# A four-layer graph network on one Trainium2 core: bias rows in two parts, late query rows on GpSimd, and the first block's chunks counted before layer 0

## The chip, the cores and the metric

The kernel runs on one core of one Trainium2 chip. Its time is the device time of one execution in microseconds (us), and of several executions the median is given. A core has five engines that run side by side, each through its own list of instructions in order: TensorE (PE in the profile; its weight loads are the rows PEld), VectorE (DVE), ScalarE (ACT), GpSimd (POOL) and SyncE (SP), which here only issues transfers. GpSimd issues transfers too, on a queue of its own. An engine waits for another through semaphores. TensorE's clock can be throttled; the profile shows the granted share.

## The reference

Input are 4096 rows x of 64 features and a 4096 x 4096 matrix adj of zeros and ones (about one in a thousand is a one). Four layers follow each other, each of the form `x = x + layer(max(layernorm(x), 0))`:

```
# layer 0: hyperbolic attention
h = lorentz_linear(h, W, b, scale)          # time column and 63 space columns
q = lorentz_linear(h, Wq, bq, scale_q);  k = lorentz_linear(h, Wk, bk, scale_k)
qm = concatenate([-q[:, :1], q[:, 1:]])
att = adj * sigmoid((2 + 2 * qm @ k.T) / att_scale + att_bias)
support = att @ h
out = support / sqrt(max(|inner(support)|, 1e-8))
# layer 1: weighting by rank
rank = cumsum(adj != 0, axis=1);  deg = rank[:, -1:];  k = minimum(deg, 100)
pos = rank - (deg - k)
w = where(adj != 0 and pos > 0, 0.5 ** (k - pos), 0);  out = w @ (h @ weight) + bias
# layer 2: 1 - 0.1 h - 0.01 * sum(h * (adj @ h))
# layer 3: relu(concatenate([h, adj @ h / max(deg, 1)]) @ W.T)
```

`lorentz_linear` multiplies by a weight, adds a bias row, takes the sigmoid of the first column as "time", and scales the other columns by a factor per row so that the row lies on a hyperboloid.

For layer 1 a row's neighbours are numbered from the last one backwards, so the kernel counts the ones of adj in chunks of 128 neighbours ahead of the numbering inside a chunk.

## The kernel before

**Tiling.** The 4096 neighbours lie in NT = 32 tiles of 128 on the partitions; the 4096 rows that are computed lie in NIB = 8 blocks of IB = 512 columns. For each block the mask, adj as FP8 of 128 x 32 x 512, is loaded by GpSimd's queue (L226, two tiles a load, converted from float32 on the way) and kept for all layers. `load_masks` issues the loads in the order in which layer 0 uses the blocks, 7 down to 0.

**Prologue and first block** (`first_rows_and_block`, L1089). Before any attention the 4096 rows need layer norm, h, q and k. They are done in two groups of 16 tiles (rows 16 to 31 first, then 0 to 15), each described by `before0` (L593) as a list of parts: VectorE means and factors, ScalarE squares and copies out of PSUM, PE transposes (`turned_half`, L678) and products (`product`: a product of bias rows with ones, L719, then products with the weight, L727), GpSimd the time column of h (L854) and of q and k (`qk_times`, L903). The rows of q and k are `qk_rows` (L892): one instruction for eight tiles, the unscaled rows tq times a factor per row, and half u of a group is turned into keys kt by transposes. The first group computes q and k rows on VectorE, the second its key rows on VectorE and its two query rows on GpSimd. Into the same list go the attention tiles of block 7, which needs all keys but only the queries of its own rows (in the first group, upper half), the query transposes of blocks 7 and 6 (`queries_turned`, L989, `queries_laid` on ScalarE), and 40 mask loads.

**The order of all that** is written out: `ORDER` is a tuple of part numbers. `Listing.run` walks through it, gives each part a planned start by planned durations, chooses for PSUM tiles among named places ("pm", "pa", "ps", "pp0", "pp1"), and issues each part on its engine. Where PE has planned idle time ahead of a part, `fill` (called for every part) issues products of ones into a tile `idle` that nobody reads (L1178), 43 at the start and afterwards `int((part.idle - 0.1) / 0.215)`, until the first attention scores. These fillers keep PE busy.

**Bias rows** (`bias_rows`, L493, GpSimd). The three bias vectors of h, q and k (192 columns) are brought as three BF16 parts that add up to float32, in three rounds: cast (L503), multiplication by a selecting column (L505), sum (L507) and remainder (L509), and the last cast to `brow` (L510). Every product of h, q or k starts with `brow`.

**Attention** is a chain for each pair of neighbour tiles: scores on PE (L1053), sigmoid on ScalarE (from PSUM), multiplication by the mask on VectorE (`att`), product with h on PE (L1084, `acc`). After block 7 a loop does blocks 6 to 0; in each turn it issues a score tile, a mask load (`load_masks(1)`), and one step of the jobs pushed earlier: the finished block's rows (`rows0`), the next block's query transposes, and the constants for layer 1 (`count_constants`, L923, pushed once after block 7, where VectorE also clears the tile `lane` and sets its middle column). The pool `pro` of the prologue is closed before the loop, and the masks of blocks 3 to 0 (`mask_b`) take its room.

**Layer 1** starts with `chunks_counted` (L1377), once for blocks 0 to 3 (quad 0) and once for 4 to 7: for each of the 32 chunks, four products of `lane` with a block's mask (L1382), 32 x 512 results each, in four groups of partitions of one PSUM bank. ScalarE copies that to `many`; `numbered` makes of `many` the numbers that go into two mask rows by transfers (L1472), and `counted` (L1495) and `products` (L1530) do the layer. Layers 2 and 3 share their products with adj (`both_layers`, L1627).

Of the kernel before, what the change touches and what calls it, by code (L numbers as in the profile page):

```python
# [10 lines left out]
F32 = mybir.dt.float32  # L11
# [13 lines left out]
D = 64  # L25
# [21 lines left out]
    206, 207, 205, 209, 208, 203, 210, 0, 1, 2, 3, 5, 4, 7, 9, 6, 8, 10, 213, 64, 11, 12, 14, 15,  # L47
    204, 13, 16, 18, 17, 211, 216, 65, 66, 67, 68, 69, 70, 19, 71, 217, 20, 21, 72, 214, 73, 127,
    74, 75, 76, 22, 79, 24, 23, 212, 215, 26, 218, 77, 78, 81, 25, 27, 28, 219, 80, 83, 82, 84,
    29, 31, 30, 85, 87, 33, 34, 32, 86, 221, 89, 88, 35, 36, 220, 37, 38, 90, 91, 222, 39, 40, 92,  # L50
    41, 43, 93, 94, 45, 96, 95, 97, 44, 223, 98, 47, 49, 100, 224, 46, 225, 42, 99, 102, 48, 101,
    50, 51, 52, 53, 60, 103, 104, 106, 56, 108, 110, 54, 57, 128, 105, 55, 61, 107, 129, 109, 111,
    62, 133, 228, 63, 161, 112, 113, 134, 149, 226, 114, 162, 230, 121, 115, 130, 150, 145, 146,
    163, 157, 151, 116, 131, 153, 119, 137, 138, 123, 124, 232, 135, 132, 164, 152, 120, 139, 158,
    136, 122, 154, 169, 147, 233, 173, 155, 170, 177, 174, 229, 165, 117, 231, 234, 156, 166, 58,
    59, 148, 159, 160, 167, 118, 235, 178, 140, 179, 236, 237, 125, 141, 126, 189, 193, 171, 142,
    143, 181, 238, 190, 185, 239, 172, 186, 191, 192, 144, 175, 176, 187, 241, 194, 195, 200, 182,
    201, 197, 240, 180, 198, 183, 184, 202, 242, 199, 196, 188, 227, 168,
# [35 lines left out]
def kernel(  # L94
# [52 lines left out]
    part = cpool.tile([P, QUAD], BF16, name="part")  # L147
    exp_s = cpool.tile([P, 3], F32, name="exp_s")
# [33 lines left out]
    def model(general):  # L182
# [55 lines left out]
        (nc.vector if general else nc.gpsimd).memset(apart_m.bitcast(I32), 0)  # L238
        q_sb = s2a.rearrange("p t k d -> p t (k d)").bitcast(F32)
# [239 lines left out]
        ppro = pool("pp_p", 1, pro_stack, space=PSUM)  # L479
# [13 lines left out]
        def bias_rows():  # L493
            v = vec[:, V_B : V_B + 3 * D]
            sel = pro.tile([P, 3], F32, name="sel" + sfx)
            high = pro.tile([P, 3 * D], BF16, name="high" + sfx)
            left, part = (
                pro.tile([P, 3 * D], F32, name=f"brow_{a}{sfx}") for a in ("left", "part")
            )
            total = pro.tile([P, 3 * D], F32, name="brow_sum" + sfx)  # L500
            nc.gpsimd.tensor_tensor(sel, ident[:, 0:3], ident[:, D : D + 3], ALU.add)
# [8 lines left out]
            nc.gpsimd.tensor_copy(brow, total)  # L510
# [74 lines left out]
        tables, flats = [], []  # L585
# [7 lines left out]
        def before0(todo, gr, bias):  # L593
# [141 lines left out]
            for u in HALF:  # L735
                pairs = [(k, k) for k in range(u * HK, (u + 1) * HK)]
                hs.append(
                    add(
                        "PE", 1.3 if u == 0 else 1.05, product("ht", pairs, 1, W_L, u == 0, "h"), ht[u], *hs, bias,
                        **({"takes": ("ps", "pp1")} if u == 0 else {}),  # L740
                    )
                )
# [124 lines left out]
            def q_out(u):  # L867
                def emit(_):
                    if u == 0:
                        v.tq = buffer("C", "tq", [P, len(HALF), 2, 2 * HK, D])  # L870
# [3 lines left out]
            for u in HALF:  # L874
# [3 lines left out]
                        "PE", 1.3, product("hq", pairs, 2, W_QK, True, f"q{u}"), hq[u],  # L878
# [35 lines left out]
            for u in reversed(HALF):  # L914
                if lead:
                    q = add("DVE", 0.65, qk_rows(u, 0, nc.vector), rq)
                else:
                    q = add("POOL", 1.35, qk_rows(u, 0, nc.gpsimd), rq)
                fq[u] = add("POOL", 0.3, qk_times(u, 0), q)
# [3 lines left out]
        def count_constants():  # L923
# [23 lines left out]
            dve.memset(lane, 0.0)  # L947
            dve.memset(lane[:, NT - 1 : NT], 1.0)
# [140 lines left out]
        def first_rows_and_block():  # L1089
# [4 lines left out]
            bias = add("POOL", 8.1, lambda _: bias_rows(), at=6.5)  # L1094
            made = [before0(listing, gr, bias) for gr in range(len(ROWS))]
# [14 lines left out]

            for ib in (last, last - 1):
# [3 lines left out]
                )  # L1115
                asked[ib] = add(
# [46 lines left out]

            for n in range(0 if general else len(todo) * EARLY // NIB * 5 // 8):
                add("POOL", 0.56, lambda _: load_masks(1), at=2.2 * max(n - 5, 0))

            v.idle = pps[0].tile([P, CG, IB], F32, tag="pp", name="idle" + sfx)
            v.filling = 0

            def fill(part):  # L1170
                if part.engine != "PE" or v.filling is None:
                    return
                if part.form == "scores":
                    v.filling = None
                    return
                for _ in range(int((part.idle - 0.1) / 0.215) if v.filling else 43):
                    v.filling += 1
                    nc.tensor.matmul(  # L1178
                        v.idle[:, v.filling % CG, :], ones,
# [8 lines left out]
        with tc.manual_schedule():  # L1188
            acc, late = first_rows_and_block()
            push(rows0(order0[0], evacuated(order0[0], acc, 0)), 10)  # L1190
            pro_stack.close()
            mp1 = pool("mask_b", 1, side="right")
            for ib in order0[EARLY:]:
                get_mask(mp1, ib)
# [16 lines left out]
            for size in sizes:  # L1211
                now = []
                for n, (ib, g) in enumerate(todo[k : k + size]):
# [10 lines left out]
                    k += 1  # L1224
                    if k == 92 and not general:
# [151 lines left out]
        def chunks_counted(quad, meanwhile):  # L1377

            pc = bank(3 + quad, f"many{quad}")
            for t in range(NT):  # L1380
# [526 lines left out]
```

## Time and profile before

| | |
|---|---|
| median of 3 runs | 569.07 us (568.34 to 570.71) |
| profiled execution | 568.73 us, of it span 567.0 us |
| mean granted clock of TensorE in the span | 0.994 |
| PE busy | 544.4 us, 3335 products |
| VectorE, ScalarE, GpSimd busy | 468.2, 357.1 and 280.2 us |
| first attention score | 44.88 us after the span's start |
| start of the copy that ends layer 0's first block | 79.21 us |
| chunk counting (L1382) | first start 292.2, last start 307.6 us |

The span is the time between the first and the last instruction that the profiler records. Each line of a timeline has the start, the time from the first to the last of its instructions, the engine, the source line, the operation with output and inputs, the shape, and the number of instructions; in square brackets stands the idle time ahead of it on that engine, with what ended it. A chain of waits is followed back from the last instruction: at each step to what released it, or to the instruction ahead of it on its engine. Busy time of PE counts fillers as well, so a busy PE of the prologue does not mean useful work.

### The profile page before, as it was taken

To read this page: it belongs to the slowest core of one execution; us is meant where nothing else is said; L and a number is where in the kernel's file an instruction comes from. 1 tells how busy PE (TensorE), PEld (TensorE's weight loads), DVE (VectorE), ACT (ScalarE), POOL (GpSimd) and SP (SyncE) were. 2 spreads that over 40 slices of the span, in tenths; PEclk is the share of its full clock that TensorE was granted. 3 is DMA by queue.
4 is the path that set the end of the run, shared out by engine and by line. 5 is a ranking of instruction groups with operands and counts; after the bars stand their busy time and mean duration, and the time that the engine had idled before them with its cause. 6 is when DMAs were issued, how large, how long until landed. Compare 5 with 4: busy or idle time off the path is not lost.

```text
span 567.0 us, 9853 instructions
## 1 busy us (share of the span) xinstructions
PE 544.4 (96%) x3335; PEld 279.5 (49%) x3335; DVE 468.2 (83%) x949; ACT 357.1 (63%) x651; POOL 280.2 (49%) x538
## 2 busy tenths in 40 slices
PE   8898999999999999999999999999999999999995
PEld 3553333333333333332334445445454888888884
DVE  5788866899998999898965977778969897789992
ACT  3589577667766758778632888988888332342231
POOL 8626614666867575754345400475644442234332
PEclk9899999999999999999999999999999999999998
DMA  8983992798999999993234255443534778859960
GB/s 141 146 82 32 86 96 20 84 145 142 166 153 148 170 151 172 130 156 97 92 123 136 102 201 163 141 153 116 173 125 149 251 266 294 281 173 328 353 242 21
DMA packets 45612, 87.86 MB, mean 155 GB/s; under 512 B 6272, under 2 KB 24576, under 8 KB 45552
## 3 DMA queue, kind: packets, MB, share of 16 engines
q1 hardware_dynamic: 26112, 69.14, 36.3%
q0 software_dynamic: 18912, 17.77, 33.5%
q8 instruction: 28, 0.46, 0.3%
q10 hardware_dynamic: 528, 0.23, 0.2%
q14 instruction: 32, 0.26, 0.1%
HBM read 135.60 MB, written 1.05 MB: 241 GB/s over the span
## 4 chain that ended last, share of the span: by engine, by line
PE 63%; DVE 14%; POOL 8%; DMA 7%; ACT 4%; issue 3%; SPq 0%; ACTq 0%; DVEq 0%; POOLq 0%
PE acc L1627 15%; PE acc L1084 13%; PE ps L1053 12%; PE acc L1530 8%; PE cnt L1495 8%; DVE att L88 4%; DMA mask<-adjt_dram 3%; DVE ckw L88 2%; POOL mask L226 2%; PE many L1382 1%; DMA s2a<-adjt_dram 1%; DVE s2a L88 1%; PE idle L1178 1%; DMA vec<-vecs_dram 1%; ACT w L88 1%
## 5 line engine op out<-in xcount | busy, mean ns | idle before, releaser
L1053 PE MATMUL ps<-qt,kt 64*128 64x512 f32 x512 | 122.3, 608 | 3.6 <-DVE att L88 3.3
L1084 PE MATMUL acc<-att,fb 128*64 128x512 f32 x512 | 117.1, 599 | 0.5 <-DVE att L88 0.5
L1627 PE MATMUL acc<-s,mask 128*128 128x256 f16 x1024 | 114.0, 273 | 0.4 <-DVE s L88 0.4
L88 ACT ACTIVATE w<-cnt 128x512 int16<-128x512 f32 x187 | 98.7, 606 | 13.0 <-PE cnt L1495 12.1
L1627 PEld LDWEIGHTS <-mask 128*128 128x128 fp8e4 x1024 | 99.8, 98 | 12.9 <-issue 1.0
L88 DVE TENSOR_TENSOR att<-ps,mask 128x1024 f32<-128x1024 f32 x82 | 98.6, 1218 | 9.1 <-ACT ps L88 8.9
L88 DVE SCALAR_TENSOR_TENSOR ckw<-ckw 128x1024 f32<-128x1024 f32 x76 | 96.0, 1273 | 4.0 <-DMA ckw<-adjt_dram 4.0
L88 ACT ACTIVATE ps<-ps,att_c,att_a 128x1024 f32<-128x1024 f32 x82 | 93.8, 1176 | 1.1 <-PE ps L1053 0.7
L88 ACT ACTIVATE att<-ps,att_c,att_a 128x1024 f32<-128x1024 f32 x46 | 54.4, 1203 | 53.0 <-PE ps L1053 48.6
L1053 PEld LDWEIGHTS ps<-qt,kt 64*128 64x128 f32 x512 | 46.1, 186 | 77.5 <-issue 30.2
L226 POOL DMA_DIRECT2D mask<-adjt_dram x128 | 70.3, 562 | 11.0 <-DMA mask<-adjt_dram 9.5
L1495 PE MATMUL cnt<-mask,after 128*128 128x512 fp8e4 x256 | 67.4, 379 | 3.6 <-DMA mask<-two 1.3
L88 DVE TENSOR_TENSOR att<-att,mask 128x1024 f32<-128x1024 f32 x46 | 57.2, 1263 | 14.6 <-ACT att L88 11.2
L1084 PEld LDWEIGHTS acc<-att,fb 128*64 128x64 f32 x512 | 33.8, 136 | 71.6 <-issue 68.4
L1530 PE MATMUL acc<-w,s2a 128*128 128x512 bf16 x256 | 66.2, 379 | 1.2 <-ACT asb L88 1.2
L88 DVE TENSOR_SCALAR w<-cnt 128x512 int16<-128x512 f32 x69 | 46.9, 686 | 23.2 <-PE cnt L1495 22.6
L316 POOL TENSOR_TENSOR rs_a<-rs_y 128x4 f32<-128x4 f32 x48 | 19.1, 398 | 67.6 <-DVE rs_y L88 61.1
L88 DVE SCALAR_TENSOR_TENSOR ck<-ck 128x512 f32<-128x512 f32 x60 | 42.8, 714 | 0.8 <-DMA ck<-adjt_dram 0.8
L1530 PEld LDWEIGHTS <-s2a 128*128 128x128 f16 x256 | 24.7, 98 | 33.6 <-issue 5.6
L88 ACT ACTIVATE xm<-xm,inn 128x64 f32<-128x64 f32 x32 | 10.4, 347 | 47.3 <-DVE high L88 45.1
L1495 PEld LDWEIGHTS <-after 128*128 128x128 bf16 x256 | 24.5, 99 | 31.8 <-issue 2.7
L88 DVE SCALAR_TENSOR_TENSOR s2a<-s2a 128x1024 f32<-128x1024 f32 x22 | 27.7, 1268 | 1.8 <-DMA s2a<-adjt_dram 1.8
(248 smaller groups left out, 611.3 us busy)
## 6 DMA issues: line engine op xcount, KB each, us to landing
ckw<-adjt_dram SPq DMA_DIRECT2D x76, 512.0 KB, 4.4
mask<-adjt_dram POOLq DMA_DIRECT2D x128, 128.0 KB, 8.6
ck<-adjt_dram SPq DMA_DIRECT2D x60, 256.0 KB, 6.0
s2a<-adjt_dram SPq DMA_DIRECT2D x22, 512.0 KB, 4.9
x_sb<-x_dram SPq DMA_DIRECT2D x4, 256.0 KB, 7.5
out_dram<-y POOLq DMA_DIRECT2D x15, 64.0 KB, 3.7
apart_m<-mask SPq DMA_DIRECT2D x16, 16.0 KB, 4.5
mask<-apart_m SPq DMA_DIRECT2D x16, 16.0 KB, 4.7
```

Of the source, the lines that this page charges most:

```text
L88: return op(out, *args, **kw)
L226: nc.gpsimd.dma_start(out=masks[ib][:, g * CG : (g + 1) * CG, :], in_=adjt[ib, g])
L316: nc.gpsimd.tensor_tensor(a, y, y, ALU.mult)
L1053: nc.tensor.matmul(ps[:, c, :], kt[half, g, :], qts[ib][half, :], start=True, stop=True)
L1084: nc.tensor.matmul(acc[c * D : (c + 1) * D, :], lhs[:, t, :], rhs[:, c, :], start=(at == 0), stop=(at == NG - 1), skip_group_check=True,)
L1178: nc.tensor.matmul(v.idle[:, v.filling % CG, :], ones, ones.unsqueeze(1).to_broadcast([P, IB // P, P]), start=True, stop=True, skip_group_ ...
L1382: nc.tensor.matmul(pc[q * NT : (q + 1) * NT, :], lane[:, NT - 1 - t : 2 * NT - 1 - t], masks[quad * QUAD + q][:, t, :], start=(t == 0), st ...
L1495: nc.tensor.matmul(cnt, by, what, start=True, stop=True, skip_group_check=True)
L1530: nc.tensor.matmul(accs[ib], apart_s if t < 0 else both(s2a, t), w, start=(t == NT - 1), stop=False, skip_group_check=True,)
L1627: nc.tensor.matmul(acc[:, to, :, :].rearrange("p k d -> p (k d)"), masks[ib][:, t, c * P : (c + 1) * P], s23[:, t, :, :].rearrange("p k d ...
```

## The change

Four things are changed.

1. `bias_rows` takes a column range. The rows of h (64 columns) are one part of the list, and those of q and k (128 columns) another; h's products wait for the first alone, q's products for the second.
2. Three of the four query rows are taken out of the list: the first group's half 0 (VectorE before) and the second group's two (GpSimd before). They go, with their time column, into `queries_left` and are issued on GpSimd in the first three turns of the loop after block 7, each after that turn's mask load. The pool `pro` is closed after the third; its PSUM part is closed before the loop as it was.
3. The 32 count products of block 7, the first block, are issued by PE before layer 0, into partitions 96 to 127 of the second bank of `idle`: in the place of fillers once 63 of those are counted, and what is left of the 32 ahead of the first query transpose. ScalarE copies them to `first_many` after that transpose. In `chunks_counted` quad 1 then has three products for each chunk in place of four and fills the other 96 partitions of `first_many`. GpSimd clears `lane` at the very start, in place of VectorE in `count_constants`.
4. `ORDER` is a new tuple for the new list. By it the first query row comes ahead of the key rows on VectorE, and on ScalarE the queries of block 7 are laid ahead of the first keys, then `first_many`, then the next keys.

By the order of the changed kernel's instructions, GpSimd issues nine mask loads ahead of the h bias rows (seven ahead of all bias rows before), one between the two parts, and seven after them. PE issues 84 fillers instead of 93. Ahead of the first query transpose stand 18 counts and 17 fillers, where 13 fillers stood ahead of the first key transposes; 4 and 10 counts stand further ahead. The two fillers between the second group's q products are gone.

```
+    nc.gpsimd.memset(lane, 0.0)
+    nc.gpsimd.memset(lane[:, NT - 1 : NT], 1.0)
...
+        first_many = parts.tile([P, IB], BF16, name="first_many" + sfx)
...
-        ppro = pool("pp_p", 1, pro_stack, space=PSUM)
+        ps_stack = ExitStack()
+        ppro = pool("pp_p", 1, ps_stack, space=PSUM)
...
-        def bias_rows():
-            v = vec[:, V_B : V_B + 3 * D]
-            sel = pro.tile([P, 3], F32, name="sel" + sfx)
...
+        def bias_rows(c0, n):
+            cols = slice(c0, c0 + n)
+            v = vec[:, V_B + c0 : V_B + c0 + n]
...
+            if c0 == 0:
+                nc.gpsimd.tensor_tensor(sel, ident[:, 0:3], ident[:, D : D + 3], ALU.add)
...
-            nc.gpsimd.tensor_copy(brow, total)
+            nc.gpsimd.tensor_copy(brow[:, cols], total)
...
                 pairs = [(k, u * HK + k) for k in range(HK)]
                 qs.append(
                     add(
-                        "PE", 1.3, product("hq", pairs, 2, W_QK, True, f"q{u}"), hq[u],
+                        "PE", 1.3, product("hq", pairs, 2, W_QK, True, f"q{u}"), hq[u], bias_qk,
...
             for u in reversed(HALF):
-                if lead:
+                if lead and u == HALF[-1]:
                     q = add("DVE", 0.65, qk_rows(u, 0, nc.vector), rq)
+                    fq[u] = add("POOL", 0.3, qk_times(u, 0), q)
                 else:
-                    q = add("POOL", 1.35, qk_rows(u, 0, nc.gpsimd), rq)
-                fq[u] = add("POOL", 0.3, qk_times(u, 0), q)
+                    queries_left.append((qk_rows(u, 0, nc.gpsimd), qk_times(u, 0)))
...
-            dve.memset(lane, 0.0)
-            dve.memset(lane[:, NT - 1 : NT], 1.0)
...
-            bias = add("POOL", 8.1, lambda _: bias_rows(), at=6.5)
-            made = [before0(listing, gr, bias) for gr in range(len(ROWS))]
+            bias_h = add("POOL", 3.8, lambda _: bias_rows(0, D), at=7.2)
+            bias_qk = add("POOL", 6.2, lambda _: bias_rows(D, 2 * D), at=7.2)
+            made = [before0(listing, gr, bias_h, bias_qk) for gr in range(len(ROWS))]
...
+            def counted_early():
+                g, c = divmod(v.counted, CG)
+                t = first_cols[g] * CG + c
+                top = slice(P - NT, P)
+                nc.tensor.matmul(
+                    v.idle[top, 1, :], lane[:, NT - 1 - t : 2 * NT - 1 - t], masks[last][:, t, :],
+                    start=(v.counted == 0), stop=(v.counted == NT - 1), skip_group_check=True,
+                )
+                v.counted += 1
+
+            def counts_kept(_):
+                if not general:
+                    nc.scalar.copy(first_many[P - NT : P, :], v.idle[P - NT : P, 1, :])
...
+            add("ACT", 0.6, counts_kept, first_turn, idle_place, frees=idle_place)
...
             def fill(part):
-                if part.engine != "PE" or v.filling is None:
+                if part.engine != "PE" or v.filling is None or part is idle_place:
                     return
+                if part is first_turn:
+                    while v.counted < NT:
+                        counted_early()
...
                 for _ in range(int((part.idle - 0.1) / 0.215) if v.filling else 43):
                     v.filling += 1
+                    if v.filling > 63 and v.counted < NT:
+                        counted_early()
+                        continue
                     nc.tensor.matmul(
-                        v.idle[:, v.filling % CG, :], ones,
+                        v.idle[:, 0, :], ones,
...
+            ps_stack.close()
-            pro_stack.close()
-            mp1 = pool("mask_b", 1, side="right")
-            for ib in order0[EARLY:]:
-                get_mask(mp1, ib)
...
                     load_masks(1)
                     k += 1
+                    if queries_left:
+                        for emit in queries_left.popleft():
+                            emit(None)
+                        if not queries_left:
+                            pro_stack.close()
+                            mp1 = pool("mask_b", 1, side="right")
+                            for later_ib in order0[EARLY:]:
+                                get_mask(mp1, later_ib)
...
+            some = QUAD if general or quad == 0 else QUAD - 1
             for t in range(NT):
-                for q in range(QUAD):
+                for q in range(some):
...
-            many[quad] = work1.tile([P, IB], BF16, name=f"many{quad}{sfx}")
-            act.copy(many[quad], pc)
+            if some == QUAD:
+                many[quad] = work1.tile([P, IB], BF16, name=f"many{quad}{sfx}")
+            else:
+                many[quad] = first_many
+            act.copy(many[quad][0 : some * NT, :], pc[0 : some * NT, :])
```

## The prediction

> **What bounds the kernel now.** I read the engines' shares first, then the chain of waits of the first 110 us, then the timeline of that stretch, and last the timeline around the chunk counting, because the change touches only the prologue, the first blocks of layer 0 and that counting.
>
> The engines' shares, from the page:
>
> ```profile
> PE 544.4 (96%) x3335; PEld 279.5 (49%) x3335; DVE 468.2 (83%) x949; ACT 357.1 (63%) x651; POOL 280.2 (49%) x538
> ```
>
> TensorE (PE) is busy nearly always, so what its stream gains or loses early is carried to the end; but in the prologue many of its instructions are fillers (products of ones), so there the chain has to say what matters. The chain of waits, in order of time (start, duration, what):
>
> ```profile
> 12.81 1.78 POOL brow_part L505
> ...
> 15.35 0.70 POOL brow L510
> ...
> 16.09 0.39 PE ps_h L719 x2
> 16.48 1.88 PE ps_h L727 x32
> 18.37 4.61 PE idle L1178 x14
> ...
> 41.08 0.70 DVE kr L892
> ...
> 42.47 0.60 POOL s2a L903
> ...
> 105.33 0.11 DVE lane L88
> ```
>
> Three things stand on it: GpSimd's bias rows (7.28 to 16.05), fourteen fillers of 4.61 us, and from 29.5 to 42.5 the VectorE chain that makes the key and query rows. The timeline shows how PE lies against it (start, busy time, engine, line, count, then the wait ahead and its releaser):
>
> ```profile
> 16.09 0.39 PE L719 MATMUL ps_h<-brow,ones 64*128 64x512 bf16 x2 [1.35 <-POOL brow L510]
> 18.30 4.68 PE L1178 MATMUL idle<-ones 128*128 128x512 bf16 x14
> 37.56 0.60 PE L1178 MATMUL idle<-ones 128*128 128x512 bf16 x2
> 39.31 2.98 PE L1178 MATMUL idle<-ones 128*128 128x512 bf16 x13
> 42.53 0.66 PE L678 MATMUL pt_k<-ident,kr 128*128 128x128 f32 x4 [0.23 <-POOL kr L903]
> 43.70 1.51 ACT L88 COPY qt<-pq 64x256 f32<-64x256 f32 x4
> 44.88 3.23 PE L1053 MATMUL ps<-qt,kt 64*128 64x512 f32 x12 [0.29 <-ACT qt L88]
> 49.94 1.55 POOL L892 TENSOR_TENSOR s2a<-tq,rrq 128x512 f32<-128x512 f32 x1 [4.97 <-ACT att L88]
> 50.50 8.60 DVE L88 TENSOR_TENSOR att<-att,mask 128x1024 f32<-128x1024 f32 x6
> ```
>
> The reader is to see that the thirteen fillers at 39.31 end at 42.29, only 0.23 us before the key rows arrive: the gap was filled to the brim, with no slack for more.
>
> **The change part by part.** The profiled run took 568.73 us: span 567.0 and 1.73 around it. That is 0.34 under the median 569.07; I sum against the span and put the difference on the median. Differences under 0.5% (2.85 us) can hardly be told from none here.
>
> *Bias rows in two parts.* GpSimd now issues nine mask loads before them in place of seven, and two memsets of lane. The queue runs eight loads: the eighth's successor waits for a landing (issue at 20.23, 0.28 after the landing at 19.95). The first load is issued at 1.93 and lands at 9.13, so the ninth starts near 9.5 (0.28 later, 0.1 for the memsets), takes 0.55, and the h part starts near 10.2 instead of 7.28. It has twelve instructions of 64 columns. By the rows of 192 columns (copy 0.34, multiplication 0.77, two-input 0.54) and of 4 columns (0.20), 64 columns cost about 0.24, 0.38 and 0.31: 4 copies, 3 multiplications, 4 two-input, the selection 0.27 and eleven gaps of 0.08 make 4.5 us, so ready at 14.7. Two of the long multiplications took 1.59 and 1.77 beside VectorE's two-input instructions; so the worst bound is no gain, 16.04. I take the middle, 15.35: **-0.7** (0 to -1.4). The second part (eleven instructions of 128 columns, about 7 us by the same rows, after one more load) is ready at 22 to 23.5, and its first user, the q product, stands at 29.88: nothing, covered by 6 us; shorter cover would cost one for one. Behind it on GpSimd seven loads of 0.55 precede the time column of h (26.25 before): 23 + 3.9 is 26.9 at worst, against h rows due near 24 to 25.5; I count nothing, at most +0.7.
>
> *The clock.* The fourteen fillers at 18.30 take 4.68: the first seven stand 0.427 apart, the rest 0.216, so seven ran at half rate, worth 7 x 0.211 = 1.5. Before them PE stood still 1.23 us (12.36 to 13.58) and 1.35 (14.75 to 16.09). The second of these shrinks to about 0.6 with the earlier rows. A lone stop of 1.28 at 309.6 is followed by full rate (four products in 1.02). After the change the stops are nearer to that single one: **-1.5** taken, 0 as the other bound. The Trainium skill ("TensorE: Matmul & The Clock Gate", Part 1: The HAM clock gate) says that the clock falls back only after a whole idle window of about 3.4 us; the stops here are shorter and the rate fell all the same, so the trace disagrees. By the rule there would be nothing to fall and the same sum would stand.
>
> *Two fillers between the last q products* (0.60 at 37.56) are gone: **-0.6**. They stood at a point where PE, not VectorE, decided (no wait ahead of 38.10 but PE's own).
>
> *Counts and fillers ahead of the first query transpose.* The written order now issues there, after the last q product, 18 counts that were left over **and** 17 fillers; the planner counts the idle time of its plan into fillers without taking off the counts. 35 in place of 13. Each streams 512 columns, as a filler does: 0.216. PE's last q product ended at 39.31; less 0.7, 1.5 and 0.6 that is 36.5. 35 x 0.216 = 7.56, so PE is free at 44.07. The query row is ready earlier: it now comes ahead of the key row on VectorE (0.61) and everything before is 2.2 earlier, 43.08 - 2.8 = 40.3. So PE is late by 3.8, and the wait for the query row turns into a wait for fillers. From the query transpose (43.13) to the laid queries' start (43.70) went 0.57: they start at 44.64, take 1.51, and now the first half's keys (0.585) are laid after them: first score at 44.64 + 1.51 + 0.585 + 0.1 = 46.83, against 44.88: **+1.95** in all, with the three gains above already in it. Bounds of a count: 0.216 as above, and 0.43 if a stream of 32 columns lets the clock fall, which no row shows (the counting of L1382 always runs four beside each other).
>
> *The copy of the counts* on ScalarE, 32x512, 0.585 as the cast of `many`, stands ahead of the second half's keys and the first sigmoid: 0 to +0.6, **+0.3** taken, since PE has four score tiles to do meanwhile.
>
> *Query rows moved to GpSimd.* Two rows leave GpSimd's stretch at 49.94 and 52.64, where two mask products took 2.07 each against 1.21 otherwise, and PE waited 0.62 (52.10, for GpSimd's key column behind the row) and 0.50 (55.25, for the second product). VectorE's own row (0.68 at 59.63) goes too. From 55.75 on the chain is PE alone, so only these waits count: **-0.8**, between 0 and -1.1. The three rows now run in the next loop turns, behind mask loads that GpSimd issues there. Whoever waits: query transposes of blocks 3 and lower, far later, and the masks of the last four blocks, whose first is needed after 140 us; nothing. Beside them three mask products can each lose 0.86 (2.6 of VectorE's time); PE's whole wait for mask products in all score tiles is 3.3, so I take 0 and keep +1 as a bound. On this the Trainium skill ("SBUF — State Buffer", SBUF: two separate sides) says that a GpSimd instruction reading SBUF and a VectorE one with two SBUF inputs exclude each other for their whole duration. By that the first of the two products would have lasted 2.2, measured 2.07; the rule speaks against a move to GpSimd, and by it the three rows would cost VectorE up to 3 x 1.0 in the loop.
>
> *Lane's memsets* leave the chain at 105.33 and 105.51, with their gaps **-0.25**.
>
> *Chunk counting in layer 1.* 256 products become 224. One tile's instructions (shortest, median, longest ns, first and last start):
>
> ```profile
> L1382 PE MATMUL many<-mask,lane x256: 379/379/391, 292.2 to 307.6; 128*32 128x512 fp8e4 x128
> ```
>
> and in the timeline what follows them:
>
> ```profile
> 309.61 1.94 PE L1495 MATMUL cnt<-mask,after 128*128 128x512 fp8e4 x7 [1.28 <-DMA mask<-two]
> ```
>
> They start in fours, 3 to 4 ns apart, and the next four 0.216 later: a block's four lanes run beside each other, and three take as long as four, 32 x 0.216 = 6.9. If each product cost its share, 0.054, it would be 32 x 0.054 = 1.7. And behind them PE waits 1.28 for a transfer that starts from the other half's counts. **0** (to -0.4 past that wait).
>
> Sum: +1.95 + 0.3 - 0.8 - 0.25 = **+1.2**: 569.9 for the profiled run, **570.3** on the median.
>
> **The rivals.**
> *The clock falls all the same.* The rows of h need not be earlier, and the stop of 1.23 stays. Then the seven fillers stay at half rate: +1.5, 571.8, and with no earlier bias rows 572.5. For it: the drop has two causes, and one stays.
> *A stream of counts slows itself* (the other side: slower). Counts load only a quarter of the array's columns. If 18 in a row run at 0.43 before the first query, 18 x 0.216 = 3.9 is added on the path: 574.2. It decides from the point where a count takes more than 0.3. Against it: the four-lane counting has full rate, though always four wide.
> *The extra 22 do not lie on the path.* If the query rows come later than I work out (GpSimd busy, VectorE behind), PE's 3.8 of lateness covers them: 570.3 - 3.8 = 566.5. Against it: PE alone already has 7.56 us to do from 36.5.
> *The removed quarter pays.* If a lane costs its share, -1.7: 568.6. Against it: starts in fours, and the 1.28 wait.
>
> **How the numbers follow.** Forecast 0.36 (its own range 569.2 to 572: bias rows ±0.7, copy and waits ±0.5), clock falls 0.26, slow counts 0.18, extra work hidden 0.09, quarter pays 0.11. Slower than 571.9: 0.05 of the forecast's tail, 0.17 of the second, 0.18 of the third, 0.40. Faster than 566.2: 0.06 of the hidden case (with another gain beside it) and 0.02 of the last, 0.08. The rest, 0.52, is within 0.5%. The range leaves out the hidden case and half of the slow counts: 568.0 to 574.2.
>
> **What would show it.** In the profile after: the bias product of h near 15.4; the fillers after h all 0.216 apart; 18 counts and 17 fillers between the last q product and the query transpose, 7.5 us, with no wait of PE behind them; a first score near 46.8; no GpSimd row in the first block, and mask products there of 1.2 only; L1382 as long as before, with 1.3 of waiting behind it. I am wrong if the query transpose waits for its rows, if counts are wider apart than 0.22, if mask products in the next block hold up PE, or if the counting of layer 1 is shorter by over a microsecond with nothing waiting behind it.

## The result, and the profile after

The changed kernel took 570.14 us in the median of 20 runs (568.9 to 572.19), the kernel before 567.53 in 20 runs beside them. The medians lie 2.6 us apart. The ratio over all runs is 1.0032, with a 95% interval of 1.0017 to 1.0047: some 1.8 us slower, and clear of no change, though less than the 0.5% that the prediction took as its bound. The profiled execution took 569.73 us, its span is 568.0.

The lines of its timeline that answer to those shown of before (start, busy time, engine, line, count, wait ahead and its releaser):

```profile
15.52 0.39 PE L725 MATMUL ps_h<-brow,ones 64*128 64x512 bf16 x2 [1.03 <-POOL brow L516]
17.58 3.19 PE L1209 MATMUL idle<-ones 128*128 128x512 bf16 x14
36.96 4.06 PE L1179 MATMUL idle<-mask,lane 128*32 128x512 fp8e4 x18
40.51 0.61 POOL L909 TENSOR_SCALAR s2a<-tmq 128x8 f32<-128x8 f32 x1 [5.29 <-DVE s2a L898]
40.95 3.84 PE L1209 MATMUL idle<-ones 128*128 128x512 bf16 x17
44.63 0.38 PE L993 MATMUL pq<-ident,s2a 128*128 128x128 f32 x2
47.22 2.85 PE L1057 MATMUL ps<-qt,kt 64*128 64x512 f32 x12
65.15 1.07 POOL L898 TENSOR_TENSOR s2a<-tq,rrq 128x512 f32<-128x512 f32 x1
```

The bias rows of h come 0.57 earlier (15.52 against 16.09), and the fillers after h all stand 0.216 apart. Then the 18 counts and 17 fillers run for 7.7 us, without a wait. The query row is complete at 41.12, and PE turns to it only at 44.63. The first score starts at 47.22, 2.34 later than before.

Set beside each other product by product, the two traces show where that goes: first score +2.34, end of the first block +0.75 (the copy of its sum starts at 79.96 instead of 79.21), chunk counting +0.30 (292.49 instead of 292.19). The last of these steps lies at 268.23, where the kernel before waited 0.36 for a mask product and the changed kernel does not. In layer 1 the timeline of before has the first line here, and the timeline of after the others:

```profile
302.01 6.00 PE L1382 MATMUL many<-mask,lane 128*32 128x512 fp8e4 x108
302.31 6.00 PE L1419 MATMUL many<-mask,lane 128*32 128x512 fp8e4 x81
309.90 1.94 PE L1535 MATMUL cnt<-mask,after 128*128 128x512 fp8e4 x7 [1.27 <-DMA mask<-two]
456.02 0.44 PE L1383 MATMUL ph<-ident,fa 128*128 128x128 f32 x2 [0.91 <-DVE x_sb L88]
```

For the last 27 chunks of quad 1 three lanes (81 products) take 6.00 us, exactly what four (108) took, and the wait behind them is the same (1.27 and 1.28). The last line is a wait for VectorE, which in these layers also checks entries of adj as transfers bring them; in the profiles of this study it is between nothing and 1.77 us, before it was 0.45. It makes the last half microsecond between these two executions, and since it comes and goes whatever the kernel, I count it to neither.

So the profiles differ by 1.0 us, close to the forecast of 1.2. The experiments show that the two kernels differ by more, and why the profiles hide it.

### The profile page after: what moved, and what is told of

Read it like the earlier page. It is cut to its first block, busy times and chain, and to the rows that moved or that the text cites. A ratio compares the mean times of both kernels' runs of the same rounds, so it can differ in the third digit from the quotient of the medians.

```text
span 568.0 us, 9850 instructions
## 1 busy us (share of the span) xinstructions
PE 547.3 (96%) x3326; PEld 280.4 (49%) x3326; DVE 466.7 (82%) x946; ACT 357.9 (63%) x652; POOL 280.5 (49%) x552
## 4 chain that ended last, share of the span: by engine, by line
PE 69%; DVE 12%; POOL 6%; ACT 4%; DMA 4%; issue 3%; ACTq 0%; DVEq 0%; POOLq 0%; SPq 0%
PE acc L1667 15%; PE ps L1057 14%; PE acc L1088 14%; PE acc L1570 8%; PE cnt L1535 8%; DVE att L88 3%; DVE ckw L88 2%; PE idle L1209 2%; DMA s2a<-adjt_dram 1%; PE many L1419 1%; DVE s2a L88 1%; POOL mask L228 1%; ACT ps L88 1%; DMA mask<-adjt_dram 1%; ACT w L88 1%
```

## The experiments

Each run shows the mean granted clock of every execution. It divides them into two groups, and most of what follows needs that division. These are all executions of the kernel before, in the three sets, and of the changed kernel:

| kernel | executions | clock 0.995 or less | their median | median of the others |
|---|---|---|---|---|
| before, first set | 35 | 15 | 570.53 | 566.87 |
| before, second set | 35 | 11 | 569.70 | 567.31 |
| before, third set | 35 | 12 | 569.57 | 567.30 |
| changed | 20 | 2 | 571.60 | 570.01 |
| changed, third set | 12 | 1 | 571.05 | 570.28 |

The profile of before that the prediction was made from is one of the first kind (clock 0.994). The border is rough. Every profile ends with 0.8 to 4.5 us at half rate behind PE's last product, which cost nothing and take 0.001 to 0.004 off the mean by themselves; so a mean between 0.996 and 0.999 need not mean any lost time, and a drop beside a short end can hide there.

### Bias rows in two parts alone

```
...
-            bias = add("POOL", 8.1, lambda _: bias_rows(), at=6.5)
+            bias_h = add("POOL", 8.1, lambda _: bias_rows(0, D), at=6.5)
+            bias_qk = add("POOL", 0.0, lambda _: bias_rows(D, 2 * D))
...
```

> The kernel before with the bias rows in two parts, and nothing else: seven mask loads ahead of both parts as before, every other instruction in the order of before. Theory (the bias rows hold up h's product): twelve instructions of 64 columns from 7.3 on are ready near 12, so h's bias product waits only for its transposed rows, and the products start near 14.9 instead of 16.09; PE's stop of 1.35 falls to about 0.2, and the seven fillers at half rate after h go to full rate. First score 44.88 - 1.2 - 1.5 = 42.2, or 43.7 if the clock drops all the same. Time 1.0 to 2.5 us below the kernel before. Rival (the half rate belongs to the execution and not to the stop): the rows come earlier, but the fillers stand at 0.43 in some executions whatever the rows do, and the gain is 1.2 at most. Rival (rows off the path): no change at all.

Measured: 566.96 (564.83 to 567.71), ratio 0.9978 (0.9955 to 1.0). None of 12 executions had a clock of 0.995 or less. Its timeline:

```profile
12.11 0.24 POOL L512 CAST brow<-brow_sum 128x64 bf16<-128x64 f32 x1
13.73 1.40 PE L680 MATMUL pt_h<-ident,xc 128*128 128x128 f32 x8 [0.60 <-DVE xc L88]
17.11 3.20 PE L1181 MATMUL idle<-ones 128*128 128x512 bf16 x14
42.57 3.23 PE L1055 MATMUL ps<-qt,kt 64*128 64x512 f32 x12 [0.30 <-ACT qt L88]
```

The rows are ready at 12.35, PE no longer waits for them, and no filler is at half rate. The median is 1.2 below that of all executions of before (568.12), in the range expected. Yet it equals that of the executions of before with the higher clock (566.87). What the split gains, as far as the times show, is that the other kind of execution did not occur; that h's bias product starts earlier (15.06, against 15.60 to 16.21 in the profiles with the rows in one part that leave the stop as it was) is not visible in them.

### The late query rows alone

The query rows' places in the list stay, as empty parts, so that the written order is the same.

```
...
-                if lead:
+                if lead and u == HALF[-1]:
...
+                    q = add(by, us, lambda _: None, rq)
+                    fq[u] = add("POOL", 0.3, lambda _: None, q)
+                    queries_left.append((qk_rows(u, 0, nc.gpsimd), qk_times(u, 0)))
...
```

> The kernel before with the three late query rows on GpSimd in the loop, and nothing else. Theory: first score as before (44.9); the mask products at 50.5 and 53.6 take 1.21 instead of 2.07 and PE's waits of 0.62 and 0.50 in the first block go, so the block ends 0.8 us earlier (bounds 0 and 1.1); the rows stretch up to three mask products after 60 us, which PE does not feel. Time 0.8 below before. Rival (the contention only moves): the mask products that are stretched later hold up PE there, time 0 to 1 us above before.

Measured: 567.68, ratio 1.0 (0.9971 to 1.0029); 4 of 12 executions with the lower clock, 566.66 for the others against 566.87. With an interval of 0.3% either way the times can't tell a gain of 0.8 from none; the trace decides for the rival. The profiled execution had the higher clock although its stop ahead of h is still 1.35 long, so it runs 1.37 ahead of the profile of before at the first score. In the first block the lead grows to 2.78, and until 78 us it shrinks to 1.36 again. The timeline there:

```profile
64.21 12.17 DVE L88 TENSOR_TENSOR att<-att,mask 128x1024 f32<-128x1024 f32 x8 [0.72 <-ACT att L88]
65.70 1.06 POOL L893 TENSOR_TENSOR s2a<-tq,rrq 128x512 f32<-128x512 f32 x1
67.91 2.79 PE L1088 MATMUL acc<-att,fb 128*64 128x512 f32 x12 [0.45 <-DVE att L88]
68.53 1.37 POOL L893 TENSOR_TENSOR s2a<-tq,rrq 128x512 f32<-128x512 f32 x1
71.66 1.36 POOL L893 TENSOR_TENSOR s2a<-tq,rrq 128x512 f32<-128x512 f32 x1
74.16 3.65 PE L1088 MATMUL acc<-att,fb 128*64 128x512 f32 x16 [0.52 <-DVE att L88]
```

Eight mask products take 12.17 beside the three rows, 1.52 each instead of 1.2, and PE waits for two of them. The first block gains 1.41 and the stretch behind it loses 1.42: the contention moved and was paid again.

### The changed kernel without the 17 fillers behind the counts

```
...
+                    early = NT - v.counted
...
-                for _ in range(int((part.idle - 0.1) / 0.215) if v.filling else 43):
+                for _ in range(int((part.idle - 0.1) / 0.215) - early if v.filling else 43):
```

> The changed kernel without the 17 products of ones that stand behind the 18 counts ahead of the first query transpose. Theory (too many instructions ahead of the first query): the 18 counts end near 41.0, the query row with its time column is ready at 41.1, so the query transpose starts near 41.2 instead of 44.63 and the first score near 43.9 instead of 47.28; of these 3.4 the first block keeps 1.5 to 3.4, the changed kernel having given back 1.6 in it. Time 1.5 to 3.4 us below the changed kernel, so 0 to 1.5 below the kernel before. Rival (PE's stream is not what the first score waits for): first score no earlier than 46, time as the changed kernel.

Measured: 567.6 (565.61 to 568.7), ratio to before 0.9992 (0.9969 to 1.0015), 2.5 below the changed kernel's 20 runs. Its timeline:

```profile
37.22 4.06 PE L1179 MATMUL idle<-mask,lane 128*32 128x512 fp8e4 x18
41.43 0.44 PE L993 MATMUL pq<-ident,s2a 128*128 128x128 f32 x2
44.07 2.85 PE L1057 MATMUL ps<-qt,kt 64*128 64x512 f32 x12
```

The 17 fillers were 3.67 us of PE (17 x 0.216). The first score is at 44.07, 3.15 earlier than in the profile of after; of this 2.66 is left at the end of the first block. So the fillers were on the path, most of their length.

### The changed kernel without the early counts

```
...
-            v.filling, v.counted = 0, NT if general else 0
+            v.filling, v.counted = 0, NT
...
-            some = QUAD if general or quad == 0 else QUAD - 1
+            some = QUAD
...
```

> The changed kernel without the early counts and their copy on ScalarE; layer 1 counts all four lanes again; fillers as the planner has them, 17 ahead of the first query transpose, and fillers where 14 counts stood. Theory (a lane of four is free, a copy is not): query transpose near 41.2 as in the run without the 17 fillers, the counting of layer 1 as long as in the changed kernel (6.0 us for the last 27 chunks of quad 1), and time 0 to 0.6 below the run without the 17 fillers for the copy of 0.585. Rival (the quarter of the counting pays): 1.7 above that run.

Measured: 566.32 (564.96 to 569.13), ratio to before 0.9968 (0.9942 to 0.9994). Against the run without the 17 fillers its trace leads by 0.59 before the copy of the counts and by 0.58 to 0.63 behind it; the 0.6 come from the bias rows (15.20 against 15.80), not from the counts. So the copy on ScalarE cost nothing that this trace shows, and counting four lanes takes the same 6.00 us for the last 27 chunks. The medians differ by more, 1.3. The intervals of the two ratios overlap, and the profiles of these two kernels, the lowest or second lowest of their sets, do not explain it.

### The stop ahead of h filled

```
...
+                stop = 0
+                if part.takes == ("ps", "pp1") and not v.stopped:
+                    v.stopped, stop = True, 6
-                for _ in range(int((part.idle - 0.1) / 0.215) if v.filling else 43):
+                for _ in range(int((part.idle - 0.1) / 0.215) + stop if v.filling else 43):
```

> The kernel before with six more products of ones between the first transposes and the first bias product of h, where PE stands still for 1.35 us; the bias rows stay one part. Theory (the stop ahead of h lets the clock drop in some executions): of the 35 executions of before, 15 had a mean granted clock of 0.995 or less and took 570.5 in the median, against 566.9 for the rest; with the stop filled none or one of twelve has such a clock, the fillers after h stand 0.216 apart, the first score is where it was without a drop (43.5), and the median is 566.9 to 567.2. Rival (earlier bias rows alone bring the gain): a third or more of the executions still show 0.995 or less and the median stays at 568.1. Rival (what ends low-clock executions is something else in the new order): the same as that.

Measured: 1 of 12 executions with the lower clock, against 11 of 35 of before beside it, and the fillers after h are all 0.216 apart. The median, 568.04, is not lower than that of before (1.0004, 0.998 to 1.0027): the executions with the higher clock took 567.89 against 567.31. The count speaks for the theory, with 12 executions not strongly, and the time does not follow. The profile shows one reason:

```profile
14.24 0.69 POOL L510 CAST brow<-brow_sum 128x192 bf16<-128x192 f32 x1
15.27 1.46 PE L1181 MATMUL idle<-ones 128*128 128x512 bf16 x6
16.66 0.39 PE L719 MATMUL ps_h<-brow,ones 64*128 64x512 bf16 x2
```

In this execution the bias rows were ready at 14.93, 1.1 before those of the profile of before, and no stop was left directly ahead of h's bias product: the six fillers themselves made h's product late. The first score is at 43.96, where 43.5 was expected and the profile with three lanes, of the same set, has 42.90. So the length of this stop differs between executions, and six fillers are more than some of them have room for.

### The stop lengthened

```
...
-                for _ in range(int((part.idle - 0.1) / 0.215) if v.filling else 43):
+                for _ in range(int((part.idle - 0.1) / 0.215) if v.filling else 34):
```

> The kernel before with the bias rows in two parts, but 34 instead of 43 products of ones at the start, so that PE stands still 1.9 us longer ahead of the first transposes, 2.5 in all, and nothing is later. Theory (stops of some 2.5 us in this stretch are what the clock answers to, wherever they lie): a third or more of twelve executions show a granted clock of 0.995 or less, where the same kernel with 43 had none of twelve, and the median rises by 1 to 3 us above the 566.96 of that kernel. Rival (only a stop directly ahead of h's products matters, or the rows themselves): no execution with a low clock, time as with 43.

Measured: 569.62, ratio 1.0028 (1.0002 to 1.0053), 8 of 12 executions with a clock of 0.995 or less (median 570.44; the others 568.18), where 43 fillers gave none of 12 in the first set and before beside it had 11 of 35. PE's first transposes start at 14.01, 0.3 from where they did, now behind

```profile
14.01 1.40 PE L680 MATMUL pt_h<-ident,xc 128*128 128x128 f32 x8 [2.35 <-DVE xc L88]
```

so next to nothing but the stop was changed, and the theory holds. In this profile itself the fillers ran at full rate: the drop is a matter of the execution. Taken together, the kernels that leave both stops as they were (before, late rows alone, three lanes) had 48 of 129 executions with the lower clock, those with a stop shortened or filled 7 of 128.

The profile of before shows how such an execution loses its time. By stretches of time (stretch, length, busy time and instructions of PE, PEld, DVE, ACT and POOL, then the granted clock, the share of the transfers and GB/s):

```profile
16.00:18.00 2.00, 1.91 (x34) 1.91 (x33) 1.91 (x3) 1.13 (x2) 2.00 (x5) 0.98 1.10 228
18.00:20.00 2.00, 2.00 (x9) 0.77 (x8) 0.25 (x1) 1.58 (x4) 1.79 (x4) 0.50 1.13 224
20.00:22.00 2.00, 2.00 (x8) 0.81 (x7) 1.83 (x5) 1.99 (x5) 0.53 (x1) 0.66 1.09 106
22.00:24.00 2.00, 2.00 (x15) 1.44 (x14) 1.86 (x6) 0.46 (x2) 1.02 (x2) 1.00 1.11 104
```

Half the clock for 3.41 us, from 17.93 to 21.34. The executions with clocks of 0.990 to 0.992 lost more; One such stretch takes 0.003 off the mean (half of 3.41 in 567 us), so as an estimate they had one more. No profile caught one of those, and where they lose it stays open.

The Trainium skill ("TensorE: Matmul & The Clock Gate", Part 1: The HAM clock gate) has the activity window run freely, so that the point at which the rate changes varies with where in the window the work falls. The profiles agree: in all 14 every change of rate lies a multiple of 3.41 us after the clock's first rise, and that rise came anywhere from 4.25 to 6.85 us after the span's start. By the page the half rate comes after at least one idle window. That does not agree: in the 3.41 us ahead of the drop in the profile of before PE stood still for 1.35.

Nor do the stops alone decide. The profiles of the late rows alone (stops of 0.81 and 1.35), of three lanes (1.50 and 0.31) and of the lengthened stop (1.97 of it inside one such stretch of 3.41) show no drop, while at the end of the kernels stretches with 2.05 us and more of standing still were followed by half rate, those with 1.81 and less were not. What else counts, for example how narrow the products of h are that fill the rest of the stretch, was not tested and stays open. The edge is not sharp either: the profile of the changed kernel has stops of 0.84 and 1.03, and 3 of its 32 executions had the lower clock.

### Three lanes of counting in the kernel before

```
...
+            some = QUAD if general or quad == 0 else QUAD - 1
...
-                for q in range(QUAD):
+                for q in range(some):
...
```

> The kernel before with three instead of four lanes in the chunk counting of quad 1. It leaves out the counts of block 7, whose places hold zeros, so what it computes for that block's rows in layer 1 is wrong; this prices the removal alone. Theory (lanes run beside each other): the counting ends when it did before, 6.0 us for its last 27 chunks, the wait of 1.3 for the transfers behind it stays, time as before within 0.3. Rival (a lane costs its share): the last 27 chunks take 1.5 us less, and the time is lower by what the wait behind does not take, 0.4 or more.

Measured: 569.46, ratio 1.0019 (0.999 to 1.0049), with 6 of 12 executions at the lower clock; the others 567.35, as before's 567.31. The timeline:

```profile
299.94 6.00 PE L1384 MATMUL many<-mask,lane 128*32 128x512 fp8e4 x81
307.52 1.94 PE L1500 MATMUL cnt<-mask,after 128*128 128x512 fp8e4 x7 [1.26 <-DMA mask<-two]
```

The same 6.00 us and the same wait: the fourth lane is free here.

### The late rows in other turns of the loop

```
...
-                    if queries_left:
+                    if queries_left and k - NG - 2 in (3, 9, 11):
...
```

> The changed kernel without the early counts, as in the run before, but the late query rows go to turns 3, 9 and 11 of the loop instead of 1, 2 and 3. In the run with turns 1 to 3 the lead over the kernel before shrank by 0.6 us between 60 and 75 us, while GpSimd made the rows; in the kernel before with late rows alone by 1.4. Theory (the rows hold VectorE's mask products wherever those read two SBUF tiles): later rows meet fewer of them, mostly such with one input in PSUM; the lead shrinks by 0.3 or less, first score and the rest unchanged, time 0.3 to 0.6 below the run with turns 1 to 3. Rival (the lead is lost for another reason, for example that the first block's first tiles are simply too early for what follows): the lead shrinks by the same 0.6 although no row lies there.

Measured: 568.19 (1.0001, 0.9981 to 1.0021). The first half came as expected: at 68 us the trace gains 0.46 on the run with turns 1 to 3. But rows in turns 9 and 11 come behind the finished block's row work, at 97.6 and 101.7, and there 2.2 is lost:

```profile
101.47 1.37 DVE L88 TENSOR_SCALAR tri<-ident 128x128 f32<-128x128 f32 x1
101.68 1.06 POOL L897 TENSOR_TENSOR s2a<-tq,rrq 128x512 f32<-128x512 f32 x1
104.84 1.13 PE L1056 MATMUL ps<-qt,kt 64*128 64x512 f32 x4 [1.11 <-DVE att L88]
```

An instruction of VectorE that takes 0.22 in the version with turns 1 to 3 took 1.37, the mask products behind it came late, and PE waited.

### The changed kernel again

> The changed kernel again, beside the others of this set and beside runs of the kernel before on the same chip. Theory (two effects of opposite sign): no more than two of twelve executions with a granted clock of 0.995 or less; the executions above that at 569.5 to 570.5, some 3 above those of the kernel before with such a clock (567), and in the median over all executions 1 to 2.5 above it, because a third of the executions of before lose 3 us or so to the clock. Rival (the half-rate fillers in the profile of before belong to all its executions): before and after differ by the same amount at equal clock as over all executions.

Measured: 570.32, ratio 1.0035 (1.0014 to 1.0056); 1 of 12 executions at the lower clock; the others 570.28, before's others 567.30, before over all 567.9. The theory holds: 3.0 slower at equal clock, 2.4 over all executions.

### Twenty-two more fillers in the kernel with bias rows in two parts

```
...
+                if ones_here == 13:
+                    ones_here += 22
...
```

> The kernel before with the bias rows in two parts, and 22 more products of ones ahead of the first key transposes (35 instead of 13), nothing else. Theory (fillers past the rows' arrival move the first score one for one, and the first block gives back only what its waits for GpSimd's query rows hold): first key transposes 4.5 later (22 x 0.216 less the wait of 0.23), first score near 47.1 against 42.6, of which the end of the first block keeps 3.4 to 4.5, and the time 3.4 to 4.5 above the 567 of the kernel with the parts alone, so 570.4 to 571.5. Rival (the first block absorbs a late start, as it gave back 1.4 to 1.6 in the changed kernel): 2 to 3 above.

Measured: 570.12, ratio 1.0036 (1.0017 to 1.0054), none of 12 at the lower clock. In the timeline

```profile
37.09 7.73 PE L1184 MATMUL idle<-ones 128*128 128x512 bf16 x35
44.66 0.60 PE L680 MATMUL pt_k<-ident,kr 128*128 128x128 f32 x4
46.95 3.23 PE L1055 MATMUL ps<-qt,kt 64*128 64x512 f32 x12 [0.30 <-ACT qt L88]
```

the first score is 4.38 later than with the parts alone, and the same 4.38 are still there at 117 us: the first block gives back nothing, as the theory has it. In time it is 2.8 above the executions of before with the higher clock and 3.2 above the kernel with the parts alone, between the theory's 3.4 to 4.5 and the rival's 2 to 3; the traces of layers 1 to 3 differ by up to 2 us in waits for transfers, either way, so what becomes of the remaining 1.2 is not resolved.

### The late rows in turns 1, 5 and 6, and the version without counts again

```
...
-                    if queries_left:
+                    if queries_left and k - NG - 2 in (1, 5, 6):
...
```

> The changed kernel without the early counts, with the late query rows in turns 1, 5 and 6 of the loop. With turns 3, 9 and 11 the rows left the stretch at 68 us alone, a gain of 0.46, but two of them fell beside VectorE's constants and row sums at 97 to 103 us, stretched one of those from 0.22 to 1.37 and cost 2.2. Theory (a row costs where VectorE's instruction beside it is followed closely by PE): at turns 5 and 6 GpSimd has nothing else until the first block's rows at 88 us, so the rows run at 75 to 80 us beside at most two mask products, the lead at 110 us is 0 to 0.5 larger than with turns 1 to 3. Rival (any place costs the same): no difference beyond 0.1.

> The changed kernel without the early counts, as in the first set (late rows in turns 1 to 3), once more beside the others. Theory: no more than one of twelve executions with a granted clock of 0.995 or less, first score near 43.5, median 566.0 to 567.3, 0.1 to 0.4% below the kernel before and 3 below the changed kernel. Rival (its 566.32 was the chip's): within 0.1% of the kernel before.

Measured: 566.94 (0.9985, 0.9968 to 1.0001) with turns 1, 5 and 6, and 566.81 (0.9989, 0.9972 to 1.0006) for the version without early counts. Neither the theory nor the rival of the turns held: the rows ran at 62.4, 67.0 and 69.9, earlier than I had worked out, and PE waited for a mask product:

```profile
69.23 1.08 PE L1087 MATMUL acc<-att,fb 128*64 128x512 f32 x4 [1.16 <-DVE att L88]
```

Against the trace with turns 1 to 3 this is 1.13 lost at once. In these runs a row's cost was decided by the one VectorE instruction it met. The version without counts is 0.1% below before here, with an interval that includes no change, and 0.3% in the first set, with one that does not; against the changed kernel beside it its median is 3.5 lower. No run shows it better than the bias rows in two parts alone (0.9978): the gain that can be seen is the absence of the lower clock, and what the version avoids is more fillers than the rows' arrival asks for.

## Why the prediction was right or wrong

The forecast, 570.3 and within 0.5%, was met by 570.14, and so was the order of things: fillers and counts past the query row's arrival, PE late by 3.5 (forecast 3.8), a chunk count that gains nothing. By its steps:

- *Bias rows*, -0.7: the product starts 0.57 earlier. Right in size, but in the times of executions at equal clock nothing of it is seen (566.96 with the parts alone against 566.87).
- *The clock*, -1.5: the mechanism was right in kind (a longer stop brings more such executions, a shorter one fewer), the term was not. The profile showed an execution with the drop, and the prediction took it for the kernel. In two of three executions of before there is no drop to save; at equal clock the term is 0. It came down to 38 of 105 executions, which by set take 2.3 to 3.7 more, so 0.8 to 1.6 in the mean. The rival that the clock falls all the same was met by 3 of the changed kernel's 32 executions.
- *Two fillers between q products*, -0.6: 1.94 between the two bias products before, 1.30 after. Right.
- *Counts and fillers*, first score +1.95 with the three gains in it: +2.34 against the profiled execution, since PE's last q product ended at 36.96 and not at 36.5. Against an execution of before without the drop, as in the runs with late rows alone (43.51) and three lanes (42.90), it is 3.7 to 4.3. This is the term that makes the change slower; 17 of the 35 alone are worth 2.5 of time. Each count took 0.22, so the rival of a slow stream of counts falls; and PE took up the query row 3.5 after its arrival, so the rival that the extra work is hidden falls too.
- *The copy*, +0.3: nothing measurable.
- *Query rows on GpSimd*, -0.8: the first block gave back 1.8 in the changed kernel's order and 1.4 with the late rows alone, more than forecast. The loop took 0.2 of it again in the changed kernel, 0.6 to 0.7 without the extra fillers or without the counts, and all 1.4 in the kernel before. The step that failed is "PE's whole wait for mask products in all score tiles is 3.3, so I take 0": in these last three PE did wait, 0.40 to 0.52 at a time, at the products with h (`acc`), which that sum of waits does not contain.
- *Lane's memsets*, -0.25: the trace gains 0.25 there, and 0.13 is lost again right behind.
- *Chunk counting*, 0: 6.00 against 6.00, in the changed kernel and alone.

So against the profiled execution of before the sum was right to 0.2 us. That execution had the drop, and the sum takes the drop off again as a gain, so the time of the changed kernel came out. The difference between the kernels did not: forecast +1.2, measured 2.6 between the medians, and at equal clock 3.0 (570.28 against 567.30). Without its clock term the sum is +2.7, close to that.

That the number was met so closely is luck in part. The median of the three runs of before, 569.07, stood above the 567.5 to 568.1 of later sets; by their times two of the three were probably executions with the lower clock. On a base of 567.3 the same sum would have given 568.5 (an estimate). A profile without the drop would have shown no clock to gain, and without that term the sum gives 570.0 on this base.

## What to carry to other kernels

A filler is free only until the data arrives: fill to the measured arrival, and take off what is put in its place; here 17 products of nothing cost 2.5 us. Before a stretch at half clock is counted as a gain, look at the granted clock of many executions: here it was a third of them. The query rows moved to GpSimd took their contention with VectorE along, and what they cost, 0.2 to 2.2 us, was decided by the VectorE instruction that PE waited for next.

## What was not expected of the hardware

- The clock's drop is a matter of the execution: in the kernels that leave both stops ahead of h's products as they were, 48 of 129 executions had a mean granted clock of 0.995 or less, with one of these stops shortened or filled 7 of 128, with one stop of 2.35 us 8 of 12.
- The rate changes on a grid of 3.41 us whose start differs between executions, by the clock in all 14 profiles; PE stood still for only 1.35 us of the 3.41 ahead of the drop that a profile caught.
- Beside a GpSimd instruction of 1.06 us with two inputs, a VectorE instruction with a single tile input, 128 x 128 of float32, took 1.37 instead of 0.22.
- A count, which has 32 columns of weights (the form 128*32) and streams 512 columns, took 0.22 by itself, as a filler with 128 columns of weights does, and four beside each other take no longer than one.
